# Two banded layers on one core: projections on 64 rows in pairs, with the bias in the weights

## The chip, the core and the metric

The kernel runs on one core of a Trainium2 chip. The metric is the time of one execution in device microseconds. The engines are called as in the profile: PE (TensorE matmul), PEld (TensorE weight load, recorded apart), DVE (VectorE), ACT (ScalarE), POOL (GpSimd), SP (SyncE, which here only issues DMAs).

## The reference

The input x is 512 x 512 positions with 64 channels, float32. Two layers of the same form follow each other, and each adds its result to x:

```python
xn = _ln(x, norm_scale, norm_bias)            # over the 64 channels; x is _gn(x) here
left = (xn @ Wl + bl) * mask * sigmoid(xn @ Wlg + blg)
right = (xn @ Wr + br) * mask * sigmoid(xn @ Wrg + brg)
out_gate = sigmoid(xn @ Wog + bog)
out = _banded_ingoing(left, right, 4)         # sum over 9 rows
out = _ln(out, out_norm_scale, out_norm_bias) * out_gate
return out @ Wo + bo
```

`_gn` is a group norm over all positions and groups of two channels. The five projections go from 64 to 128 channels. The banded sum takes, for output row i, the rows i-4 to i+4 of `right`, each times the entry of `left` at that row and column i: for each of the 128 hidden channels a product of a banded 512 x 512 matrix with a 512 x 512 matrix.

## The kernel before

The output rows are cut into blocks of 104 (the last has 96); 112 input rows go into each (`KIN`). Within a block the 512 columns are cut into 8 chunks of 64 columns. Two layers of five blocks of eight chunks make 80 chunks.

At the start of a block, `build_A` makes the band matrix A from `left`: 104 columns in 13 steps of 8 (`JP`). These are called band steps here. Then each chunk has two stages:

- `project` goes over its 64 columns in 8 steps of 8 columns. `transposed` turns the normalised z (rows in the partitions) on PE (line 274: four transposes, each of two columns of 64 channels, so that channels come out on 128 partitions), and ACT copies the result into the tile zT (line 281). `gated` multiplies four columns at a time with two weights side by side (line 288: the stationary operand is zT, 112 columns wide, the moving one the weights, 256 wide). ACT takes the sigmoid of one half (line 290), DVE multiplies it with the other and writes R (line 328). Line 332 makes the output gate with the gate's weights as the stationary operand and zT as the moving one, and line 337 its sigmoid.
- `mix` (line 346) multiplies A and R for each of 128 hidden channels; DVE and ACT empty PSUM into O in turns (lines 354 and 352).

`finish` is the third part. It takes the statistics of O (line 361 and the lines behind it), and then, in steps of 8 columns, normalises O (line 408, DVE), turns it (line 409, PE), scales it (line 411, ACT), multiplies it with the gates (line 412, DVE), multiplies with Wo (line 414, PE) and adds x (line 419, DVE). `together` emits `finish` of one chunk and `project` of the next in turns, so the two share a stage; `mix` stands alone. `normalised` prepares z, 16 columns at a time, over DMA, POOL, DVE and ACT, in two buffers.

The bias of a projection comes in as a 65th row: zT has a row of ones in partition 64, and the weights tile aug has the bias in partition 64. The lower 64 partitions of the transposed pair hold even columns, the upper 64 odd ones, and two ACT copies bring both to partitions 0 to 63.

A scheduler sets the order of instructions on each engine; every engine then runs its own list strictly in that order and waits where an operand is not ready. PSUM has four one-bank buffers (`one_bank`) and two of two banks (`two_banks`).

Of the kernel before, what the change touches and what calls it, by code (L numbers as in the profile page):

```python
# [8 lines left out]
F32 = mybir.dt.float32  # L9
# [47 lines left out]
class Block:  # L57
    """Rows o..o+m of the output; rows s..s+KIN go into them."""
# [9 lines left out]
def tile_two_banded_layers(  # L68
# [20 lines left out]
    # The first layer's output, less what its groups' means are near to: those of its input and  # L89
    # of the last bias. The second layer's norm does not see it, and its end adds it.  # L90
# [8 lines left out]

    def one_bank():  # L100
# [5 lines left out]
    def rsqrt(o: bass.AP, v: bass.AP):  # L106
        """o = v ** -0.5, for v > 0: a first guess from the bits of v, and Newton's steps."""
# [11 lines left out]
    def load_layer(i: int, w: dict, tmp) -> dict:  # L119
        r = {}  # L120
        raw = tmp.tile([D, 5 * H], F32, tag="raw", name=f"raw{i}")
        brow = tmp.tile([1, 5 * H], F32, tag="brow", name=f"brow{i}")
        for n, nm in enumerate(("r", "rg", "l", "lg", "og")):
            nc.sync.dma_start(raw[:, n * H : (n + 1) * H], w[f"W{nm}"])
            nc.sync.dma_start(brow[:, n * H : (n + 1) * H], row(w[f"b{nm}"]))
        ns = tmp.tile([D, 1], F32, tag="ns", name=f"ns{i}")
        nb = tmp.tile([D, 1], F32, tag="nb", name=f"nb{i}")
        nc.sync.dma_start(ns, col(w["norm_scale"]))
        nc.sync.dma_start(nb, col(w["norm_bias"]))
        aug = const.tile([D + 1, 5 * H], F32, tag=f"aug{i}", name=f"aug{i}")  # L130
        nc.vector.tensor_scalar(aug[:D, :], raw, ns, None, ALU.mult)
        for lo, hi in ((0, 4 * H), (4 * H, 5 * H)):
            pb = one_bank()
            nc.tensor.matmul(pb[:1, : hi - lo], lhsT=nb, rhs=raw[:, lo:hi], start=True, stop=True)
            nc.vector.tensor_tensor(brow[:, lo:hi], pb[:1, : hi - lo], brow[:, lo:hi], ALU.add)
        nc.sync.dma_start(aug[D : D + 1, :], brow)
# [6 lines left out]
        # To all partitions: the last bias, and the mask of the columns.  # L143
# [17 lines left out]
    def spread(o: bass.AP, v: bass.AP):  # L161
        """Values of the groups, [P, G], to their channels, [P, D]."""
# [6 lines left out]
    def group_affine(mean: bass.AP, var: bass.AP, pool):  # L169
        """From the groups' means and variances, on all partitions."""  # L170
# [351 lines left out]
```

## Time and profile before

| | |
|---|---|
| median of 2 runs | 16617.86 us (16617.22 to 16618.49) |
| profiled execution, first to last instruction | 16607.0 us; the profile gives no other time for it |
| busy time of PE | 14135.4 us |
| busy time of DVE | 9995.0 us |
| busy time of ACT | 4482.2 us |
| busy time of POOL | 4394.1 us |
| DMA | 521.69 MB, mean 31 GB/s |
| mean granted TensorE clock | 0.559 |

Rows of the grouped view read: line, engine, operation, output<-inputs, shape (for PE: rows * columns of the stationary operand, then the moving operand), count | busy us, mean ns of one | idle us of the engine before them, and what ended it. Rows of a view by stretches read: from:to in us, length, then busy us and count of PE, PEld, DVE, ACT and POOL, then the granted clock, the DMA share and GB/s. Rows of a timeline read: start, us, engine, line, operation, names, shape, count, and in brackets the idle time before it and what ended it; the us of several merged instructions run from the first start to the last end. A matmul's recorded end lies behind the start of the next, since matmuls are pipelined.

### The profile page before, as it was taken

The numbers are of one execution on the slowest core, as the hardware profiler recorded it, in microseconds if no ns is written. First come the engines' busy times: TensorE is split into PE (matmuls) and PEld (weight loads), VectorE is DVE, ScalarE is ACT, GpSimd is POOL, SyncE is SP. The second block draws the span as 40 slices with busy tenths as digits, with TensorE's granted clock in tenths as the row PEclk, the third lists the DMA queues.
The fourth block names the chain that finished last, engine by engine and source line by source line (L and its number), as shares of the span: only waits on it lengthen the run. The fifth ranks groups of instructions, "written<-read, shape, count | busy, mean of one in ns | idle before, by whom it ended". The sixth has DMA issues, their size and how long they took to land. (4 is left out here: it accounts for less than half of the span.)

```text
span 16607.0 us, 148858 instructions
## 1 busy us (share of the span) xinstructions
PE 14135.4 (85%) x53782; PEld 11229.3 (68%) x53782; DVE 9995.0 (60%) x24532; ACT 4482.2 (27%) x6982; POOL 4394.1 (26%) x2408
## 2 busy tenths in 40 slices
PE   3888888888888888888878888888888888888887
PEld 2677667666766676676657666666666766676776
DVE  7565665666566656656655555555555555556555
ACT  1222222222222222222222222222222222222222
POOL 2232422232223222422331113111311121113111
PEclk9999855555555555555555555555555555555555
DMA  4011101110111011100100111111011101110100
GB/s 177 24 30 27 30 26 28 27 31 25 28 27 31 25 27 27 31 25 26 31 25 26 27 29 29 27 29 29 27 29 29 29 26 30 27 30 27 29 27 27
DMA packets 130302, 521.69 MB, mean 31 GB/s; under 512 B 17872, under 2 KB 18522, under 8 KB 127516
## 3 DMA queue, kind: packets, MB, share of 16 engines
q1 hardware_dynamic: 129564, 512.18, 11.0%
q8 instruction: 423, 6.93, 0.2%
q14 instruction: 315, 2.58, 0.1%
HBM read 377.90 MB, written 134.22 MB: 31 GB/s over the span
## 5 line engine op out<-in xcount | busy, mean ns | idle before, releaser
L288 PE MATMUL banks<-aug,zT 65*112 65x256 f32 x12288 | 5734.7, 643 | 493.2 <-ACT zT L281 392.8
L288 PEld LDWEIGHTS banks<-aug,zT 65*112 65x112 f32 x12288 | 3619.6, 306 | 2234.2 <-ACT zT L281 629.9
L346 PE MATMUL bank<-R,A 112*104 112x64 f32 (+1 forms) x20480 | 3522.5, 378 | 4.0 <-DVE z_m L256 4.0
L346 PEld LDWEIGHTS bank<-R,A 112*104 112x104 f32 (+1 forms) x20480 | 3513.0, 290 | 16.4 <-DVE z_m L256 16.4
L414 PE MATMUL bank<-Wo,zh 128*104 128x64 f32 (+1 forms) x10240 | 1974.9, 377 | 1058.6 <-DVE zh L412 616.6
L414 PEld LDWEIGHTS bank<-Wo,zh 128*104 128x104 f32 (+1 forms) x10240 | 1899.9, 287 | 1352.1 <-issue 908.6
L252 POOL TENSOR_TENSOR z<-z,ga 112x1024 f32<-112x1024 f32 (+1 forms) x388 | 906.5, 2336 | 6161.5 <-DMA z<-mid_x 4155.6
L408 DVE TENSOR_SCALAR O<-O,o_nm,o_rs 104x128 f32<-104x128 f32 (+1 forms) x5120 | 2246.2, 490 | 0.6
L328 DVE TENSOR_TENSOR R<-banks,sg 112x512 f32<-112x512 f32 x1280 | 1321.0, 1032 | 1432.0 <-ACT sg L290 1428.8
L290 ACT ACTIVATE sg<-banks 112x512 f32<-112x512 f32 x1536 | 917.3, 597 | 4455.9 <-PE banks L288 4344.6
L354 DVE COPY O<-bank 104x512 f32<-104x512 f32 (+1 forms) x640 | 661.2, 1033 | 2292.8 <-PE bank L346 2290.8
L332 PE MATMUL bank<-zT,aug 65*128 65x416 f32 (+1 forms) x2560 | 2012.2, 889 | 0.0
L409 PEld LDWEIGHTS bank<-ident,O 104*128 104x128 f32 (+1 forms) x5120 | 959.5, 234 | 934.5 <-issue 772.1
L409 PE MATMUL bank<-ident,O 104*128 104x104 f32 (+1 forms) x5120 | 1130.4, 381 | 539.8 <-DVE O L408 539.8
L411 ACT ACTIVATE zh<-bank,ob,os 128x416 f32<-128x416 f32 (+1 forms) x1280 | 884.1, 692 | 2064.4 <-PE bank L409 2052.4
L352 ACT COPY O<-bank 104x512 f32<-104x512 f32 (+1 forms) x640 | 651.9, 1019 | 2921.8 <-PE bank L346 2921.8
L361 DVE BATCH_NORM_STATS2 o_st<-O 104x6 f32<-104x128 f32 (+1 forms) x5120 | 1136.7, 276 | 219.7 <-ACT O L352 219.7
L412 DVE TENSOR_TENSOR zh<-zh,gate 128x416 f32<-128x416 f32 (+1 forms) x1280 | 822.9, 643 | 737.6 <-ACT zh L411 729.1
L424 POOL TENSOR_TENSOR sum<-sum,xr 104x512 f32<-104x512 f32 (+1 forms) x320 | 431.5, 1348 | 2722.7 <-DVE xr L419 2064.8
L390 POOL TENSOR_TENSOR xr<-xr,add 104x1024 f32<-104x1024 f32 (+1 forms) x320 | 765.6, 2393 | 1356.0 <-DMA xr<-mid_x 798.8
L257 POOL TENSOR_TENSOR z<-z,z_m 112x1024 f32<-112x1024 f32 (+1 forms) x388 | 742.4, 1914 | 1329.9 <-DVE z_m L256 1067.7
L419 DVE TENSOR_TENSOR xr<-bank,xr 104x512 f32<-104x512 f32 (+1 forms) x640 | 441.9, 690 | 1059.9 <-PE bank L414 1052.0
(99 smaller groups left out, 10223.3 us busy)
## 6 DMA issues: line engine op xcount, KB each, us to landing
z<-in_x_dram SPq DMA_DIRECT2D x190, 448.0 KB
z<-mid_x SPq DMA_DIRECT2D x190, 448.0 KB
gn_x<-in_x_dram SPq DMA_DIRECT2D x16, 4096.0 KB
xr<-in_x_dram SPq DMA_DIRECT2D x128, 416.0 KB
mid_x<-xr SPq DMA_DIRECT2D x128, 416.0 KB
xr<-mid_x SPq DMA_DIRECT2D x128, 416.0 KB
out_dram<-xr SPq DMA_DIRECT2D x128, 416.0 KB
xr<-in_x_dram SPq DMA_DIRECT2D x32, 384.0 KB
```

The costliest lines, as they stand in the source:

```text
L252: nc.gpsimd.tensor_tensor(z, z, mid(ga[:KIN], n), ALU.mult)
L288: nc.tensor.matmul(pr[:KIN, q, :], lhsT=t[:, j + q, :], rhs=w, start=True, stop=True)
L290: nc.scalar.activation(sg, pr[:KIN, :, H:], AF.Sigmoid)
L328: nc.vector.tensor_tensor(R[:KIN, :, jr : jr + JQ].rearrange("p h j -> p j h"), v, sg, ALU.mult)
L332: nc.tensor.matmul(pg, lhsT=w["gate"], rhs=t[:, q : q + JQ, blk.off : blk.off + blk.m], start=True, stop=True,)
L346: nc.tensor.matmul(pb[:, h, :], lhsT=A[:KIN, h0 + h, : blk.m], rhs=R[:KIN, h0 + h, :], start=True, stop=True,)
L361: nc.vector.bn_stats(st[:, j, :], O[:m, j0 + j, :])
L408: nc.vector.tensor_scalar(oj, oj, nm[:, js], rs[:, js], ALU.add, ALU.mult)
L409: nc.tensor.transpose(pt[:, k * m : (k + 1) * m], oj, ident[:m, :m])
L411: nc.scalar.activation(zh, pt, AF.Identity, bias=w["ob"], scale=w["os"])
L412: nc.vector.tensor_tensor(zh, zh, gates[(j0 + q) // JQ], ALU.mult)
L414: nc.tensor.matmul(po[:, q + k, :], lhsT=zh[:, k * m : (k + 1) * m], rhs=w["Wo"], start=True, stop=True,)
```

## The change

Products use 64 rows of the array instead of 65. The transposed pair of columns stays where the transposes put it, even columns in partitions 0 to 63 and odd ones in 64 to 127, and one ACT instruction takes all 128 partitions. The weights lie twice in aug, once in each half, and the products of an even and an odd column alternate; those of even columns go to one PSUM bank of the pair, those of odd columns to the other.

The bias has no row any more. z has zero mean over its 64 channels, so the mean over the channels can be taken from each column of the weights without changing the product. ACT adds 1 to z on its way into zT, and the centred weights get the bias divided by 64 in each row: the ones times the weights then give the bias. The setup works this out with the block-diagonal tile half.

Since even and odd columns come apart, R and A are written in two DVE instructions, two columns each, where one wrote four, and the POOL multiplication of the band is split in the same way. The output gates of a step are made after both groups of products, one for the four even columns and one for the four odd ones, and `finish` takes the columns in that order.

Line numbers move: 274 becomes 289, 281 becomes 294, 288 becomes 306, 290 becomes 311, 328 becomes 354, 332 becomes 361, 337 becomes 366, 346 becomes 375, 361 becomes 390, 408 becomes 437, 409 becomes 438, 411 becomes 440, 412 becomes 441, 414 becomes 443.

```diff
     def load_layer(i: int, w: dict, tmp) -> dict:
...
-        raw = tmp.tile([D, 5 * H], F32, tag="raw", name=f"raw{i}")
+        raw = tmp.tile([P, 5 * H], F32, tag="raw", name=f"raw{i}")
...
+        for e in range(2):
+            part = slice(e * D, (e + 1) * D)
+            for n, nm in enumerate(("r", "rg", "l", "lg", "og")):
+                nc.sync.dma_start(raw[part, n * H : (n + 1) * H], w[f"W{nm}"])
...
-        aug = const.tile([D + 1, 5 * H], F32, tag=f"aug{i}", name=f"aug{i}")
-        nc.vector.tensor_scalar(aug[:D, :], raw, ns, None, ALU.mult)
+        nc.vector.tensor_scalar(brow, brow, 1.0 / D, None, ALU.mult)
+        hb = tmp.tile([P, P], F32, tag="hb", name=f"hb{i}")
+        nc.vector.tensor_scalar(hb, half, nb, None, ALU.mult)
+        aug = const.tile([P, 5 * H], F32, tag=f"aug{i}", name=f"aug{i}")
+        nc.vector.tensor_scalar(aug, raw, ns, None, ALU.mult)
         for lo, hi in ((0, 4 * H), (4 * H, 5 * H)):
-            pb = one_bank()
-            nc.tensor.matmul(pb[:1, : hi - lo], lhsT=nb, rhs=raw[:, lo:hi], start=True, stop=True)
-            nc.vector.tensor_tensor(brow[:, lo:hi], pb[:1, : hi - lo], brow[:, lo:hi], ALU.add)
-        nc.sync.dma_start(aug[D : D + 1, :], brow)
+            pm = one_bank()[:, : hi - lo]
+            nc.tensor.matmul(pm, lhsT=half, rhs=aug[:, lo:hi], start=True, stop=True)
+            pb = one_bank()[:, : hi - lo]
+            nc.tensor.matmul(pb, lhsT=hb, rhs=raw[:, lo:hi], start=True, stop=False)
+            nc.tensor.matmul(pb, lhsT=ones_row, rhs=brow[:, lo:hi], start=False, stop=True)
+            nc.vector.tensor_tensor(aug[:, lo:hi], aug[:, lo:hi], pm, ALU.subtract)
+            nc.vector.tensor_tensor(aug[:, lo:hi], aug[:, lo:hi], pb, ALU.add)
...
-    zT = [keep.tile([D + 1, JP // 2, 2, KIN], F32, name=f"zT{i}") for i in range(2)]
-    for t in zT:
-        nc.vector.memset(t[D : D + 1, :, :, :], 1.0)
+    zT = [keep.tile([P, JP // 2, KIN], F32, name=f"zT{i}") for i in range(2)]
...
     def transposed(z: bass.AP, j: int):
...
-        pt = pt[:, : JP // 2 * KIN].rearrange("q (k p) -> q k p", p=KIN)
-        for e in range(2):
-            nc.scalar.copy(t[:D, :, e, :], pt[e * D : (e + 1) * D])
-        return t.rearrange("c k e p -> c (k e) p")
+        nc.scalar.activation(
+            t.rearrange("c k p -> c (k p)"), pt[:, : JP // 2 * KIN], AF.Identity, bias=1.0
+        )
+        return t
 
     def gated(t: bass.AP, j: int, w: bass.AP):
-        pr = two_banks()
-        for q in range(JQ):
-            nc.tensor.matmul(pr[:KIN, q, :], lhsT=t[:, j + q, :], rhs=w, start=True, stop=True)
...
+        pr = two_banks().rearrange("p (e k) h -> p e k h", e=2)
+        for k in range(JQ // 2):
+            for e in range(2):
+                part = slice(e * D, (e + 1) * D)
+                nc.tensor.matmul(
+                    pr[:KIN, e, k, :], lhsT=t[part, j // 2 + k, :], rhs=w[part],
+                    start=True, stop=True,
+                )
...
     def build_A(zs, w: dict, mask: bass.AP, blk: Block):
...
-                    nc.gpsimd.tensor_tensor(sg, sg, last(b[:, i : i + JQ], H), ALU.mult)
-                    nc.vector.tensor_tensor(
-                        A[:KIN, :, i : i + JQ].rearrange("p h i -> p i h"), v, sg, ALU.mult
-                    )
+                    for e in range(2):
+                        nc.gpsimd.tensor_tensor(
+                            sg[:, e], sg[:, e], last(b[:, i + e : i + JQ : 2], H), ALU.mult
+                        )
+                        nc.vector.tensor_tensor(
+                            A[:KIN, :, i + e : i + JQ : 2].rearrange("p h k -> p k h"),
+                            v[:, e], sg[:, e], ALU.mult,
+                        )
...
     def project(zs, w: dict, blk: Block, gates: list):
...
-                    nc.vector.tensor_tensor(
-                        R[:KIN, :, jr : jr + JQ].rearrange("p h j -> p j h"), v, sg, ALU.mult
-                    )
-                    pg = one_bank()[:, : JQ * blk.m].rearrange("h (j p) -> h j p", p=blk.m)
+                    for e in range(2):
+                        nc.vector.tensor_tensor(
+                            R[:KIN, :, jr + e : jr + JQ : 2].rearrange("p h k -> p k h"),
+                            v[:, e], sg[:, e], ALU.mult,
+                        )
+                for e in range(2):
+                    part = slice(e * D, (e + 1) * D)
+                    pg = one_bank()[:, : JQ * blk.m].rearrange("h (k p) -> h k p", p=blk.m)
                     nc.tensor.matmul(
-                        pg, lhsT=w["gate"], rhs=t[:, q : q + JQ, blk.off : blk.off + blk.m],
+                        pg, lhsT=w["gate"][part], rhs=t[part, :, blk.off : blk.off + blk.m],
...
     def finish(src: bass.AP, dst: bass.AP, w: dict, blk: Block, c: int, gates: list, stats: bool):
...
-            for q in range(0, JP, JQ):
+            for e in range(2):
...
-                    j = j0 + q + k
+                    j = j0 + 2 * k + e
```

The scheduler puts the instructions nearly as before. These are the rows of PE in one step of the first layer, a finish step woven into a project step, before (L409 and L414 belong to the finish, the others to the projection):

```order
L409 MATMUL bank<-ident,O 128x104 x4
L274 MATMUL bank<-ident,z 128x112 x4
L288 MATMUL banks<-aug_101,zT_808 112x256
L414 MATMUL bank<-Wo_110,zh 104x64 x4
L288 MATMUL banks<-aug_101,zT_808 112x256 x3
L332 MATMUL bank<-zT_808,aug_101 128x416
L288 MATMUL banks<-aug_101,zT_808 112x256 x4
L332 MATMUL bank<-zT_808,aug_101 128x416
L409 MATMUL bank<-ident,O 128x104 x4
L414 MATMUL bank<-Wo_110,zh 104x64 x4
```

and in the changed kernel:

```order
L438 MATMUL bank<-ident,O 128x104 x4
L289 MATMUL bank<-ident,z 128x112 x4
L306 MATMUL banks<-aug_115,zT_845 112x256
L443 MATMUL bank<-Wo_131,zh 104x64 x4
L306 MATMUL banks<-aug_115,zT_845 112x256 x7
L361 MATMUL bank<-zT_845,aug_115 128x416 x2
L438 MATMUL bank<-ident,O 128x104 x4
L443 MATMUL bank<-Wo_131,zh 104x64 x4
```

The two gates have moved behind all eight products; the finish stands where it stood. L306 and L361 are of 64 rows, the rows around them of the whole array.

On DVE, at the head of a chunk's stage, the statistics of the first 32 columns of O (L361, now L390) stand between the writes of R, before:

```order
L361 BN_STATS o_st<-O 104x6 x15
L328 TENSOR_TENSOR R<-banks,sg 112x4x128
L361 BN_STATS o_st<-O 104x6 x10
L328 TENSOR_TENSOR R<-banks,sg 112x4x128
L361 BN_STATS o_st<-O 104x6 x8
```

and in the changed kernel:

```order
L390 BN_STATS o_st<-O 104x6 x15
L354 TENSOR_TENSOR R<-banks,sg 112x2x128 x2
L390 BN_STATS o_st<-O 104x6 x5
L354 TENSOR_TENSOR R<-banks,sg 112x2x128 x2
L390 BN_STATS o_st<-O 104x6 x13
```

Each write of R is two of half the size, and the second pair stands five statistics earlier.

More of the change, by code (lines that the diff above doesn't have):

```diff
@@ L98, in tile_two_banded_layers @@
     nc.vector.memset(ones_row, 1.0)
+    half = const.tile([P, P], F32, name="half")
+    nc.vector.memset(half, 0.0)
+    for e in range(2):
+        nc.vector.memset(half[e * D : (e + 1) * D, e * D : (e + 1) * D], 1.0 / D)
     def one_bank():
@@ L402, in finish @@
             po = one_bank()[:m, :].rearrange("i (j c) -> i j c", c=D)
-            for q in range(0, JP, JQ):
+            for e in range(2):
                 pt = one_bank()[:, : JQ * m]
                 for k in range(JQ):
-                    j = j0 + q + k
+                    j = j0 + 2 * k + e
                     oj, js = O[:m, j, :], slice(j % JS, j % JS + 1)
@@ L411, in finish @@
                 nc.scalar.activation(zh, pt, AF.Identity, bias=w["ob"], scale=w["os"])
[L412 removed]
+                nc.vector.tensor_tensor(zh, zh, gates[j0 // JQ + e], ALU.mult)
                 for k in range(JQ):
                     nc.tensor.matmul(
[L415 removed]
+                        po[:, 2 * k + e, :], lhsT=zh[:, k * m : (k + 1) * m], rhs=w["Wo"],
                         start=True, stop=True,
```

19 lines of the change are left out of this document (8 added, 11 removed).

## The prediction

> **What bounds the kernel now.** I read the page first, then the busy time by stretches, then TensorE's own timeline.
>
> ```profile
> span 16607.0 us, 148858 instructions
> PE 14135.4 (85%) x53782; PEld 11229.3 (68%) x53782; DVE 9995.0 (60%) x24532; ACT 4482.2 (27%) x6982; POOL 4394.1 (26%) x2408
> L288 PE MATMUL banks<-aug,zT 65*112 65x256 f32 x12288 | 5734.7, 643 | 493.2 <-ACT zT L281 392.8 <-DVE A L314 44.0 <-DVE z_r L116 25.4
> L288 PEld LDWEIGHTS banks<-aug,zT 65*112 65x112 f32 x12288 | 3619.6, 306 | 2234.2 <-ACT zT L281 629.9 <-issue 473.0 <-DVE A L314 51.8
> ```
>
> PE is busy 85%, and the largest group is the one that the change touches. The code has 6,144 of these products and the trace 12,288 records: each float32 product is two load-and-multiply records, one after the other.
>
> The stretches below are, in turn, the mixing stage of a chunk at an early and a later time, the project-and-finish stage of a chunk in the first and the second layer, and the two halves of a block's first chunk with its band.
>
> ```profile
> 649.60:695.50 45.90, 45.90 (x268) 45.90 (x267) 12.84 (x18) 8.28 (x9) 9.50 (x6) 1.00 0.08 20
> ...
> 6182.70:6228.60 45.90, 45.90 (x268) 45.90 (x267) 12.84 (x18) 8.28 (x9) 9.49 (x6) 0.50 0.07 19
> 6228.60:6372.70 144.10, 119.55 (x376) 86.70 (x376) 104.73 (x265) 45.78 (x75) 46.80 (x27) 0.50 0.12 31
> ...
> 10761.30:10904.00 142.70, 119.66 (x378) 86.87 (x377) 97.22 (x272) 41.66 (x68) 31.48 (x14) 0.50 0.12 31
> 6798.50:6935.00 136.50, 102.25 (x350) 79.18 (x349) 113.48 (x264) 39.37 (x63) 64.89 (x44) 0.50 0.11 30
> 6935.00:7063.10 128.10, 112.05 (x276) 75.71 (x276) 71.51 (x119) 39.41 (x68) 54.59 (x31) 0.50 0.11 31
> ```
>
> A chunk is 45.9 us of mixing, which the change leaves alone, and 144 us of projecting one chunk while the last one is finished. There are 80 chunks; 70 look like this and 10 open a block. The granted clock is 1.00 in the first row and 0.50 in the second, with the same 45.90 us: these matmuls do not follow it, and I give the clock no term. What ends last in the 144 us is seen in one step (8 columns) of PE's timeline:
>
> ```profile
> 6261.29 0.90 PE L409 MATMUL bank<-ident,O 104*128 104x104 f32 x4
> 6261.98 0.95 PE L274 MATMUL bank<-ident,z 112*128 112x112 f32 x4
> 6263.55 1.19 PE L288 MATMUL banks<-aug,zT 65*112 65x256 f32 x2 [0.61 <-ACT zT L281]
> 6264.54 1.52 PE L414 MATMUL bank<-Wo,zh 128*104 128x64 f32 x8
> 6265.85 2.85 PE L288 MATMUL banks<-aug,zT 65*112 65x256 f32 x6
> 6268.49 1.59 PE L332 MATMUL bank<-zT,aug 65*128 65x416 f32 x2
> 6269.88 3.62 PE L288 MATMUL banks<-aug,zT 65*112 65x256 f32 x8
> 6273.29 1.59 PE L332 MATMUL bank<-zT,aug 65*128 65x416 f32 x2
> 6274.68 0.90 PE L409 MATMUL bank<-ident,O 104*128 104x104 f32 x4
> 6277.09 1.62 PE L414 MATMUL bank<-Wo,zh 128*104 128x64 f32 x8 [1.51 <-DVE zh L412]
> 6278.50 0.90 PE L409 MATMUL bank<-ident,O 104*128 104x104 f32 x4
> ```
>
> From L409 to L409 the step takes 17.21 us, and PE's queue in order is the whole of it: the starts give 0.69 + 1.57 + 0.99 + 1.31 + 2.64 + 1.39 + 3.41 + 1.39 + 2.41 + 1.41. Two waits lie in it, for zT (inside the 1.57) and for zh (inside the 2.41). A record of L288 costs 3.41/8 = 0.426 us, one of L332 1.39/2 = 0.695 us; each ends about 0.21 us after the next has started (6269.88 + 3.62 against 6273.29), so the means on the page overstate PE. The projections are 16 x 0.426 + 4 x 0.695 = 9.6 of the 17.21 us.
>
> **Overlap of the halves.** Afterwards a product takes 64 rows, alternately the lower and the upper. The two records of one product stay in one half and must follow each other, but the second record of one product can run beside the first of the next. The order has one product alone, L443, seven products, two gates. Seven products are 14 records with 6 such meetings: 8 x 0.426 = 3.41 us, where 2.64 + 3.41 = 6.05 stood. The gates (four records of 0.695, one meeting of their own, and one with the last product) take 2.78 - 0.695 - 0.426 = 1.66 instead of 2.78. Together 3.76 us less per step. It needs the weights in time:
>
> ```profile
> 6246.31 3.62 PE L288 MATMUL banks<-aug,zT 65*112 65x256 f32 x8
> 6246.31 2.87 PEld L288 LDWEIGHTS banks<-aug,zT 65*112 65x112 f32 x7 [0.39 <-issue]
> ```
>
> Seven loads lie inside eight matmuls of the same rows, so a load runs beside the matmul ahead of it. A load that bounds its stream costs 45.90/268 = 0.171 us for 104 columns in the mixing rows, 0.184 for 112; two of them, 0.37, fit beside one record of 0.426. That two halves compute at once is shown by no row: the gain lies between 0 and 3.76, and I take the upper end: by the code the two products of a pair have their own partitions of zT and of the weights and their own PSUM bank, so that no data or buffer makes one wait for the other.
>
> [...]
>
> **Changes of tile size.** Products and gates now stand in another tiling than everything else on PE. Counted in the changed order, PE changes 2,248 times, four times in such a step; the one between L289 and L306 lies in the wait for zT. The nearest row is in the setup:
>
> ```profile
> 8.92 2.29 PE L134 MATMUL bank<-raw,nb 64*1 64x512 f32 x4 [8.92 <-DMA Wo<-in_L_conv_Wo_dram]
> 11.13 0.69 PE L151 MATMUL bank<-bo,ones_row 1*128 1x64 f32 x2
> ```
>
> L134 (64 rows) ends at 11.21 and L151 (1 row) starts at 11.13, 0.08 us before that end, where 0.21 is usual: 0.13 us lost. Behind a stop the first record also shows its load: L288 x2 lasts 0.99 above, 0.14 over 2 x 0.426. I take 0.27 us for each of three changes, 0.81 per step. Bounds: 0.13, and the whole tail with a whole load, 0.21 + 0.306 = 0.52.
>
> [...]
>
> **One copy instead of two, two products instead of one.**
>
> ```profile
> L328 DVE TENSOR_TENSOR R<-banks,sg 112x512 f32<-112x512 f32 x1280 | 1321.0, 1032 | 1432.0 <-ACT sg L290 1428.8
> ...
> L281 ACT COPY zT<-bank 64x448 f32<-64x448 f32 x1536 | 812.3, 529 | 187.7 <-PE bank L274 146.6
> ...
> L337 ACT ACTIVATE gate<-bank 128x416 f32<-128x416 f32 x1024 | 529.6, 517 | 742.5 <-PE bank L332 607.8 <-DVE zh L412 133.3
> ...
> L114 DVE TENSOR_TENSOR rsqrt<-z_r 112x16 f32<-112x16 f32 x1140 | 256.9, 225 | 13.3
> ```
>
> Two copies of 529 ns on 64 partitions become one on 128. The nearest row on 128, L337, takes 517, so PE's wait for zT shrinks by one copy, 0.53 us. R's evacuation becomes two of 256 elements. If DVE's time were all elements nothing would be added; if all of the 225 ns of a 16-element row were fixed, 0.22 each. I take 0.15: 0.3 us per step, 2.4 per chunk of DVE. The band's multiplications on POOL and DVE split alike, in 128 of 768 steps. The setup gets more loads and matmuls in front of the first transfer of x; the loads of now end by 8.92, so 0 to 10 us, taken as 5.
>
> **What the path keeps.** PE's step: 17.21 - 3.76 - 0.53 + 0.81 = 13.7 us, 3.5 less. But now DVE is near. Its busy time in the six steps behind the head:
>
> ```profile
> 6262.54:6279.75 17.21, 15.09 (x50) 11.06 (x49) 12.51 (x32) 5.30 (x10) 2.48 (x2) 0.50 0.01 1
> 6279.75:6296.97 17.22, 15.10 (x51) 11.07 (x49) 13.81 (x30) 5.32 (x10) 9.73 (x6) 0.50 0.29 77
> 6296.97:6315.65 18.68, 15.09 (x51) 11.08 (x49) 14.70 (x41) 6.14 (x11) 4.17 (x3) 0.50 0.00 1
> 6315.65:6328.35 12.70, 12.09 (x35) 8.35 (x33) 10.51 (x12) 4.10 (x8) 7.13 (x4) 0.50 0.39 103
> 6328.35:6345.00 16.65, 13.72 (x43) 9.63 (x41) 15.91 (x36) 5.06 (x9) 4.21 (x2) 0.50 0.00 0
> 6345.00:6362.00 17.00, 14.39 (x46) 10.36 (x46) 4.97 (x7) 4.97 (x9) 9.01 (x5) 0.50 0.10 28
> ```
>
> With 0.3 added, DVE (the third busy column) lets these steps save 3.5, 2.9, 3.5, 1.8, 0.4 and 3.4 us: 15.5, of which I keep 13 for queueing in its strict order. The second layer, with 97.22 instead of 104.73 us of DVE, keeps about 17 of 5 x 3.5 + 4.4. Ahead of the steps lies the head:
>
> ```profile
> 6228.39 0.95 PE L274 MATMUL bank<-ident,z 112*128 112x112 f32 x4
> ...
> 6239.80 0.95 PE L274 MATMUL bank<-ident,z 112*128 112x112 f32 x4
> ...
> 6256.46 1.11 PE L409 MATMUL bank<-ident,O 104*128 104x104 f32 x4 [5.15 <-DVE O L408]
> ```
>
> Two steps of 11.41 us run without a finish, then PE waits for DVE. A step there sheds 7 x 0.426 = 2.98, 1.12 on the gates and 0.53, and pays one change: 4.4 us. DVE's statistics, in turn, wait for the next z, whose buffer the second step frees; so the head gives one step's gain, 4.4, and the rest is waited away.
>
> A common chunk saves 17.4 in the first layer and 21.4 in the second, 19.4 on the mean. A block's first chunk: its first half is DVE's already (113.48 of 136.5), 3 us; in the second, eight steps without a finish at 4.4 and about three of the band at 3.2 make 45, of which I take three quarters, 33, since z tiles come from a chain over DMA, POOL, DVE and ACT that gets no faster. So 70 x 19.4 + 10 x 36 - 5 = 1,713 us off the profiled 16,607.0. The runs' median lies 11 us above that span: 14,894 + 11, say **14,900 us**. Its own range, with 12 to 27 us per common chunk and 20 to 50 per first one: 14,250 to 15,600.
>
> **Rivals.**
> *The weights come late.* For: no row shows a load passing a waiting matmul of the other half. Then each product's start waits for one load behind the last record: a pair of products takes 2 x (0.426 + 0.184) = 1.22, where now 1.70 and ideally 0.85. That is 56% of 3.76; a step saves 2.1 + 0.53 - 0.81 = 1.8, a chunk 10, a first chunk 20: 900 us, 15,720. Were a half's own load (0.306) never hidden, a pair takes 1.46, a step saves 0.8, a chunk about 5: 16,150. Against: the overlap of loads shown. Chance 0.13. [...]
>
> *DVE takes the step over.* For: 15.91 of 16.65. If POOL's interference and the extra instructions leave a chunk 9 and a first chunk 20: 15,790. Against: 4.97 of 17.00 one step on. Chance 0.09.
>
> *The halves do not compute at once* (the change doesn't do what it says). Then only the copies and the changes of tiling count: -768 x 0.53 = -407, and 2,248 x 0.27 = +607: 16,820, within 2% (332 us, about what a measurement of this kernel can tell from no change). Chance 0.09.
>
> *The same, and each change of tiling drains and reloads*, on the other side: 2,248 x 0.52 = 1,169 - 407 = +762, 17,380. It decides from (332 + 407)/2,248 = 0.33 us a change; were the halves to overlap it would take 1.2 us. For it: nothing in the steady stages shows a change yet. Against: 0.13 us in the setup. Chance 0.15.
>
> **Chances and range.** Forecast 0.54, the first two rivals 0.22: faster 0.76; within 2% 0.09; slower 0.15. Leaving out the slow case and the low tail, the range is 14,250 to 16,900.
>
> **What would show it.** Starts of neighbouring L306 records about 0.43 us apart in pairs that coincide, 3.4 us for seven products, prove the overlap; even spacing of 0.426 refutes it, 0.6 between pairs means late weights. L306 to L443 shows the price of a change. L289 to L306 should be 1.04 us. Steps of 13.7 us prove the sum; steps of 16 with DVE busy throughout prove DVE. What would make it wrong at once is a period of a chunk of 190 us or more.

## The result, and the profile after

The changed kernel takes 15059.37 us (median of 2 runs, 15052.18 to 15066.56) against 16617.86: a ratio of 0.9063, 95% interval 0.9037 to 0.9089. The forecast was 14,900 us. The profiled execution's span went from 16607.0 to 15064.8 us, 1,542 us less, where the sum had 1,713.

From the page of the changed kernel, the span and the busy time of the engines:

```profile
span 15064.8 us, 150188 instructions
...
PE 10365.6 (69%) x53798; PEld 8549.5 (57%) x53798; DVE 9972.1 (66%) x26077; ACT 3944.5 (26%) x6214; POOL 4445.0 (30%) x2664
```

PE is busy 3,770 us less, and less than half of that is gone from the span. DVE, which did not change, is now at 66%, about level with PE. The grouped view shows the products, and the two instructions that write R and normalise O:

```profile
L306 PE MATMUL banks<-aug,zT 64*112 64x256 f32 x12288 | 2973.0, 599 | 986.5 <-ACT zT L294 358.3 <-DVE R L354 232.0 <-DVE A L338 165.6
L437 DVE TENSOR_SCALAR O<-O,o_nm,o_rs 104x128 f32<-104x128 f32 (+1 forms) x5120 | 2244.9, 488 | 1.6
L354 DVE TENSOR_TENSOR R<-banks,sg 112x256 f32<-112x256 f32 x2560 | 1321.9, 589 | 209.5 <-ACT sg L311 205.2
```

The products fell from 5,734.7 to 2,973.0 us of busy time. R's 2,560 half writes cost 1,321.9 us, where 1,280 whole ones cost 1,321.0: splitting them was free.

The stretches of the changed kernel that answer to those of before: the mixing, the project-and-finish stage in the first and in the second layer, and a block's first chunk with its band in one row.

```profile
5722.60:5768.50 45.90, 45.90 (x267) 45.90 (x266) 12.77 (x18) 8.40 (x9) 9.55 (x6) 0.50 0.07 20
5768.50:5899.70 131.20, 80.52 (x377) 59.36 (x376) 103.04 (x281) 40.16 (x67) 46.82 (x27) 0.62 0.12 33
10043.30:10165.50 122.20, 78.07 (x378) 57.52 (x377) 96.05 (x288) 35.67 (x60) 31.59 (x14) 0.61 0.13 36
6301.10:6528.80 227.70, 122.72 (x626) 85.98 (x624) 188.59 (x421) 65.44 (x110) 124.47 (x99) 0.63 0.13 35
```

Mixing stays at 45.90 us. The first layer's stage went from 144.1 to 131.2 us, the second's from 142.7 to 122.2, the first chunk's two stretches from 136.5 + 128.1 to 227.7. In the first layer PE is busy for only 80.5 of 131.2 us: it waits. The granted clock, 0.50 in these stages before, is now 0.6 on the mean in those with projections.

PE's timeline at the start of such a stage and in one step of it:

```profile
5770.03 3.76 PE L306 MATMUL banks<-aug,zT 64*112 64x256 f32 x16 [0.74 <-ACT zT L294]
5773.58 1.60 PE L361 MATMUL bank<-zT,aug 64*128 64x416 f32 x4
5775.11 0.78 PE L289 MATMUL bank<-ident,z 112*128 112x112 f32 x4
5776.62 1.98 PE L306 MATMUL banks<-aug,zT 64*112 64x256 f32 x16 [0.73 <-ACT zT L294]
5778.44 0.86 PE L361 MATMUL bank<-zT,aug 64*128 64x416 f32 x4
...
5796.18 0.90 PE L438 MATMUL bank<-ident,O 104*128 104x104 f32 x4
5796.87 0.95 PE L289 MATMUL bank<-ident,z 112*128 112x112 f32 x4
5798.46 1.19 PE L306 MATMUL banks<-aug,zT 64*112 64x256 f32 x2 [0.63 <-ACT zT L294]
5799.58 1.65 PE L443 MATMUL bank<-Wo,zh 128*104 128x64 f32 x8
5801.15 3.33 PE L306 MATMUL banks<-aug,zT 64*112 64x256 f32 x13
5803.85 0.90 PE L361 MATMUL bank<-zT,aug 64*128 64x416 f32 x1
5804.27 0.63 PE L306 MATMUL banks<-aug,zT 64*112 64x256 f32 x1
5804.55 1.74 PE L361 MATMUL bank<-zT,aug 64*128 64x416 f32 x3
5806.22 0.58 PE L438 MATMUL bank<-ident,O 104*128 104x104 f32 x4
5809.96 1.62 PE L443 MATMUL bank<-Wo,zh 128*104 128x64 f32 x8 [3.15 <-DVE zh L441]
5811.37 0.90 PE L438 MATMUL bank<-ident,O 104*128 104x104 f32 x4
```

Sixteen records take 3.55 us from start to start (5770.03 to 5773.58): eight times 0.427 and a change of tiling, so the halves compute at once from the first record to the last. One step later the same sixteen take 1.82 us. That is about half of it, and nothing in the code differs. In the step from 5796.18 to 5811.37 the projections, which there run at the old rate, cost what was forecast, but the wait for zh has grown from 1.51 to 3.15 us. These two readings, the halved records and the longer waits, are what the experiments were for.

### The profile page after: what moved, and what is told of

Its sections match the earlier page's. It is cut to its first block, busy times and chain, and to the rows that moved or that the text cites. A ratio compares the mean times of both kernels' runs of the same rounds, so it can differ in the third digit from the quotient of the medians.

```text
span 15064.8 us, 150188 instructions
## 1 busy us (share of the span) xinstructions
PE 10365.6 (69%) x53798; PEld 8549.5 (57%) x53798; DVE 9972.1 (66%) x26077; ACT 3944.5 (26%) x6214; POOL 4445.0 (30%) x2664
## 5 line engine op out<-in xcount | busy, mean ns | idle before, releaser
L306 PE MATMUL banks<-aug,zT 64*112 64x256 f32 x12288 | 2973.0, 599 | 986.5 <-ACT zT L294 358.3
L375 PE MATMUL bank<-R,A 112*104 112x64 f32 (+1 forms) x20480 | 3522.2, 378 | 64.1 <-DVE R L354 64.1
L443 PE MATMUL bank<-Wo,zh 128*104 128x64 f32 (+1 forms) x10240 | 1955.4, 373 | 2039.2 <-DVE zh L441 842.6
L443 PEld LDWEIGHTS bank<-Wo,zh 128*104 128x104 f32 (+1 forms) x10240 | 1766.8, 276 | 2464.1 <-issue 1834.0
L306 PEld LDWEIGHTS banks<-aug,zT 64*112 64x112 f32 x12288 | 1761.5, 273 | 1706.7 <-ACT zT L294 598.5
L437 DVE TENSOR_SCALAR O<-O,o_nm,o_rs 104x128 f32<-104x128 f32 (+1 forms) x5120 | 2244.9, 488 | 1.6
L438 PE MATMUL bank<-ident,O 104*128 104x104 f32 (+1 forms) x5120 | 1013.8, 348 | 1085.5 <-DVE O L437 1085.1
L438 PEld LDWEIGHTS bank<-ident,O 104*128 104x128 f32 (+1 forms) x5120 | 800.1, 207 | 1448.0 <-issue 1041.7
L354 DVE TENSOR_TENSOR R<-banks,sg 112x256 f32<-112x256 f32 x2560 | 1321.9, 589 | 209.5 <-ACT sg L311 205.2
L390 DVE BATCH_NORM_STATS2 o_st<-O 104x6 f32<-104x128 f32 (+1 forms) x5120 | 1134.7, 278 | 221.0 <-ACT O L381 221.0
L441 DVE TENSOR_TENSOR zh<-zh,gate 128x416 f32<-128x416 f32 (+1 forms) x1280 | 765.9, 601 | 486.2 <-ACT zh L440 478.2
L274 ACT ACTIVATE sq<-z 112x1024 f32<-112x1024 f32 (+1 forms) x388 | 405.7, 1046 | 2013.0 <-POOL z L272 2010.3
```

The source lines that it names most:

```text
L306: nc.tensor.matmul(pr[:KIN, e, k, :], lhsT=t[part, j // 2 + k, :], rhs=w[part], start=True, stop=True,)
L354: nc.vector.tensor_tensor(R[:KIN, :, jr + e : jr + JQ : 2].rearrange("p h k -> p k h"), v[:, e], sg[:, e], ALU.mult,)
L375: nc.tensor.matmul(pb[:, h, :], lhsT=A[:KIN, h0 + h, : blk.m], rhs=R[:KIN, h0 + h, :], start=True, stop=True,)
L390: nc.vector.bn_stats(st[:, j, :], O[:m, j0 + j, :])
L437: nc.vector.tensor_scalar(oj, oj, nm[:, js], rs[:, js], ALU.add, ALU.mult)
L438: nc.tensor.transpose(pt[:, k * m : (k + 1) * m], oj, ident[:m, :m])
```

## Experiments

| run | what differs | us | mean granted clock |
|---|---|---|---|
| e1_lower_half | all products on the same 64 rows | 16864.08 | 0.502 |
| e2_full_rows | products on 128 rows, half of them zeros | 15134.47 | 0.677 |
| e3_wide_mix | changed kernel, mixing 104 columns wide | 13481.39 | 0.691 |
| e7_mix_80 | the same, 80 wide | 15067.10 | 0.593 |
| e11_mix_92 | the same, 92 wide | 13656.39 | 0.670 |
| e6_before_wide_mix | kernel before, mixing 104 wide, first run | 31340.35 | 0.581 |
| e9_before_wide_again | kernel before, mixing 104 wide | 14781.88 | 0.605 |
| e10_rows_wide | e2 and e3 together | 13654.66 | 0.763 |
| e5_no_sums | changed kernel without POOL's sums | 14668.04 | 0.595 |
| e4_act_norm | half of O's normalisation on ACT | 14567.49 | 0.600 |
| e8_wide_act | e3 and e4 together | 13009.87 | 0.691 |
| e12_wide_act34 | e8 with three quarters on ACT | 12864.32 | 0.689 |

Where the text gives no number of runs, the time is that of a single one. Time ahead of a trace's first clock record counts as 1.00 in the means (12,958 us of e6, under 0.5 ms elsewhere in the table).

The theories: the halves overlap (the forecast), or the gain comes from somewhere else; and the part of the gain that is missing is PE's own, or DVE's, or comes from POOL.

**Is it the overlap? All products on the lower rows.** ACT makes two copies, one for each parity, both into partitions 0 to 63; every product and gate uses those rows.

```diff
-    zT = [keep.tile([P, JP // 2, KIN], F32, name=f"zT{i}") for i in range(2)]
+    zT = [keep.tile([D, 2, JP // 2, KIN], F32, name=f"zT{i}") for i in range(2)]
...
-                    pr[:KIN, e, k, :], lhsT=t[part, j // 2 + k, :], rhs=w[part],
+                    pr[:KIN, e, k, :], lhsT=t[:, e, j // 2 + k, :], rhs=w[:D],
```

> The changed kernel with every product on the lower 64 rows, and with two copies into zT as before; the bias stays in the weights, and the order and the changes of tiling stay. Theory (the gain is the overlap of the two halves): without a second half at work the records of L306 follow each other at 0.43 us, PE pays 2,248 changes at about 0.14 to 0.27 us for nothing, and the time is 16,700 to 17,000. Rival (the gain comes from fewer waits and the new order of gates): most of the gain stays, 15,300 to 15,600.

16864.08 us. PE's timeline of this run, and that of the weight loads:

```profile
6005.66 7.17 PE L306 MATMUL banks<-aug,zT 64*112 64x256 f32 x16
6005.66 6.42 PEld L306 LDWEIGHTS banks<-aug,zT 64*112 64x112 f32 x16
```

Sixteen records take 7.17 us instead of 3.76: one after the other, each 0.427. The gain is gone when the halves are gone. The loads of these records (the second row) stay hidden beside the products though all use the same rows (6.42 us of loads within the 7.17), which speaks against the rival in which a half's own load is never hidden.

**Or the share of the array? 128 rows, no halves.** The weights stand twice in a zero-padded tile, so that a product takes all 128 rows of zT and the zeros drop the other column. Nothing overlaps and no tiling changes.

```diff
+        pad = const.tile([P, 2, 5 * H], F32, tag=f"pad{i}", name=f"pad{i}")
+        nc.vector.memset(pad, 0.0)
+        for e in range(2):
+            part = slice(e * D, (e + 1) * D)
+            nc.vector.tensor_copy(pad[part, e, :], aug[part, :])
...
-                    pr[:KIN, e, k, :], lhsT=t[part, j // 2 + k, :], rhs=w[part],
+                    pr[:KIN, e, k, :], lhsT=t[:, j // 2 + k, :], rhs=w[:, e, :],
```

> The changed kernel with products over all 128 rows: the weights lie twice, each time with zeros in the other half, so there is no change of tiling and no pair, but one copy into zT, the halved writes of R and the gates at the end of the step stay. One gate buffer fewer, to make room. Theory (overlap): products are serial again, a common chunk sheds 8 x 0.5 us of the copy, 16,250 to 16,400, with L306 at 0.43 us. Rival (the gain is the full clock, which PE is granted once all of its rows are in use): L306 falls to 0.21 us for part of the time here too, the granted clock rises to 0.6 or more, and the time is 15,000 to 15,500.

15134.47 us, only 75 us more than with the halves. PE's timeline, two steps in turn:

```profile
5809.38 5.82 PE L311 MATMUL banks<-pad,zT 128*112 128x256 f32 x16 [0.74 <-ACT zT L300]
...
5817.64 3.71 PE L311 MATMUL banks<-pad,zT 128*112 128x256 f32 x16 [0.66 <-ACT zT L300]
```

The first sixteen records begin at 0.427 us each and end at 0.216, the second sixteen run at 0.216 throughout. So TensorE does have a faster rate here, twice the usual one, and full rows reach it with zeros in half of them. In this trace the clock's own records show 1.00 in 556 windows, 5,339 us in all; in the changed kernel in 581 windows of 3.4 to 13.7 us, 2,761 us; in the kernel before in three, 17 us. The change thus brings two things, an overlap that holds at either clock (sixteen records in 3.55 us at 0.50, in 1.82 at 1.00) and bursts of the full clock. The full clock without the overlap brings nearly the same time; whether the overlap alone would is not shown, and how much of the 1,542 us is the clock's share was not separated: no run had the overlap at 0.50 throughout. The trace of the changed kernel bounds it. A fifth of L306's records (2,512 of 12,288) start at 1.00, where 7,293 do with full rows, and PE is busy for 1,068 of the 2,761 us at 1.00. Even if all of that would have taken twice as long at 0.50 (an estimate), at least some 2,700 of the 3,770 us that PE is busy less are not the clock's.

**Does the mixing follow the clock?** It is 45.9 us of every chunk, and if the share of the array in use decides, it should be possible to raise it. In the changed kernel each mixing product now reads 104 moving columns instead of 64; the 40 more land where the next product of the bank writes, which overwrites them.

```diff
-                    pb[:, h, :], lhsT=A[:KIN, h0 + h, : blk.m], rhs=R[:KIN, h0 + h, :],
+                    pf[:, h * JC : h * JC + n], lhsT=A[:KIN, h0 + h, : blk.m],
+                    rhs=Rf[:KIN, (h0 + h) * JC : (h0 + h) * JC + n],
```

with n = 104, and 64 for the last product of a bank.

> The changed kernel with 104 instead of 64 moving columns in the mixing products: the 40 further columns are written over by the next product of the same bank, so that the output is the same. The records are bound by their weight loads of 104 columns, so that this costs nothing by itself. If the granted clock follows how much of the array is in use: the mixing stage (0.50 now) gets the full clock, 45.9 us become 23 to 30, and the time is 13,300 to 14,000. If it does not: 45.9 us as before, 15,050 to 15,150.

13481.39 us, 1,578 us faster for 40 useless columns. PE's timeline of a mixing stage in this run:

```profile
4839.42 3.54 PE L378 MATMUL bank<-R,A 112*104 112x104 f32 x20
...
4843.49 21.80 PE L378 MATMUL bank<-R,A 112*104 112x104 f32 x236
```

Twenty records at 0.17 us, the old rate, then 236 at 0.092. Where the change of rate lies, the next two runs narrow down (the same edit with other widths):

> As the changed kernel with the wide mix, but with 80 moving columns instead of 104. Of the array's rows times columns times time, mixing then uses 112/128 x 80/128 = 0.55, where 64 columns use 0.44 and 104 use 0.71. If the clock goes up where a threshold under 0.55 is passed: about 13,480 as with 104. If the threshold is above: 15,060. In between, if the share of windows with the full clock follows the use gradually: 13,900 to 14,700.

> The changed kernel with mixing products of 92 moving columns. 80 columns gave nothing (15067 us), 104 gave 13481 us. Rows x columns in use times the share of time: 112/128 x 92/104 of the time of a weight load is 0.77 against 0.67 (80) and 0.875 (104). Theory A, a limit below 0.77: mixing runs at the full clock, near 13,500 us. Theory B, a limit above it: mixing stays at 0.173 us a record, 15,070 us. Anything between would mean that the clock goes up and down within a mixing stage.

```profile
L378 PE MATMUL bank<-R,A 112*104 112x92 f32 (+3 forms) x20480 | 2159.0, 275 | 54.8 <-DVE R L354 54.8
```

80 columns change nothing (15067.1 us); 92 do nearly all of it (13656.39 us, the grouped row above, against 3,522.2 us for the mixing of the changed kernel). At the old rate a record takes 0.17 us with 64 moving columns and with 104, so the load of 104 columns sets it. A loaded column then costs 0.171/104 = 1.65 ns, a moving one 0.427/256 = 1.67 ns (from L306), so 80 columns keep the array computing about 77% of the time, 92 columns 88% (an estimate from these two). The step lies between.

**The same edit on the kernel before.** A first run of it took 31340.35 us. Its page shows the clock by slices, and the products:

```profile
PEclk9999999999999999622222222222222222333333
...
L288 PE MATMUL banks<-aug,zT 65*112 65x256 f32 x12288 | 11794.5, 1221 | 384.3 <-ACT zT L281 381.8 <-DVE A L314 2.5
```

> The kernel before with 104 instead of 64 moving columns in its mixing products, nothing else. Theory (full clock once enough of the array is in use, whatever else the kernel does): mixing falls from 45.9 to about 24 us, the projections stay at 0.43 us a record, since they use 65 rows, and the time is 14,700 to 15,000. Rival (it takes the pairs of halves in the stage before to raise the clock): 16,600.

The records of L288 are spaced 1.28 us at first, then 0.84 and at last 0.62, where 0.427 is usual; the 9s stand where no grant was recorded (the first 12,958 us), and the two grants on record behind that are 0.26 and 0.36. The same code was run once more:

> The kernel before with mixing products of 104 moving columns, once more. The earlier run of the same code took 31340 us, with a clock of a quarter to a third where it was recorded. Theory A, that slowness belonged to that run: mixing goes to the full clock as in the changed kernel with the same edit (0.092 us a record instead of 0.173), a chunk loses 15 to 22 us, 80 chunks 1,200 to 1,800 us: 14,800 to 15,400 us. Theory B, it belongs to this program: 31,000 us again, with the projections' records of 65 rows spaced 1.28 us at first and 0.6 to 0.85 later.

14781.88 us (2 runs; ratio 0.8897, 95% interval 0.8871 to 0.8922). So the slowness does not belong to the program. The repeat ran on another chip, and other programs had their usual times on the first one; what caused it stays open. PE's timeline of the repeat, a mixing stage and the projections behind it:

```profile
5205.04 21.80 PE L349 MATMUL bank<-R,A 112*104 112x104 f32 x236
...
5228.31 2.10 PE L288 MATMUL banks<-aug,zT 65*112 65x256 f32 x8 [1.08 <-ACT zT L281]
...
5263.06 3.62 PE L288 MATMUL banks<-aug,zT 65*112 65x256 f32 x8
```

With the projections of before, one edit in the mixing gains more than the whole change: the mixing runs at the full clock, the first products behind it too (eight records in 2.10 us), later ones at 3.62 as ever. The change is worth 1,300 us on top of it (14,782 to 13,481).

**Do the halves still count at the full clock?** Full rows and wide mixing together:

> Full 128-row products one after the other (no overlap, no change of tile size) with the mixing products at 104 moving columns. The pairs with the same mixing took 13481 us. Theory A, the clock carries the gain and the overlap hardly counts, since DVE sets the step once PE runs at the full clock: 13,450 to 13,700 us. Theory B, the overlap is a gain of its own on top of the clock: seven products cost 14 x 0.213 instead of 8 x 0.213 us and the gates two records more, about 1.8 us a step less 0.4 us of tile changes at the higher clock, 768 steps: 13,481 + 1,000, 14,300 to 14,700 us.

13654.66 us (ratio 0.8218, 95% interval 0.8194 to 0.8242), 173 us above the halves with the same mixing: theory A. In the grouped view PE's largest wait of this run ends with DVE:

```profile
L451 PE MATMUL bank<-Wo,zh 128*104 128x64 f32 (+1 forms) x10240 | 1777.0, 347 | 1710.9 <-DVE zh L449 1325.6 <-DVE z_v L284 161.2 <-DVE z_m L277 148.4
```

With the pairs (e3) the products are busy for 1,018 us less (2,850.4 instead of 3,868.5), and PE waits 326 us longer at that place (2,036.9 instead of 1,710.9).

**What holds the first layer back: POOL's sums.** The two additions that POOL makes per step in the first layer are left out except in the first step of a block; the running sums, and so the second layer's group norm, are not the reference's.

```diff
-                nc.gpsimd.tensor_tensor(sum1[:m], sum1[:m], f, ALU.add)
-                nc.gpsimd.tensor_tensor(sum2[:m], sum2[:m], s2, ALU.add)
+                if c == 0 and j0 == 0:
+                    nc.gpsimd.tensor_tensor(sum1[:m], sum1[:m], f, ALU.add)
+                    nc.gpsimd.tensor_tensor(sum2[:m], sum2[:m], s2, ALU.add)
```

The reason to suspect them stands in DVE's timeline of the changed kernel,

```profile
5807.96 1.35 DVE L437 TENSOR_SCALAR O<-O,o_nm,o_rs 104x128 f32<-104x128 f32 x5
...
5824.56 1.22 DVE L270 TENSOR_REDUCE z_m<-z 112x16 f32<-112x1024 f32 x1 [2.57 <-POOL z L268]
5825.70 0.58 DVE L441 TENSOR_TENSOR zh<-zh,gate 128x416 f32<-128x416 f32 x1
...
5849.40 7.54 DVE L437 TENSOR_SCALAR O<-O,o_nm,o_rs 104x128 f32<-104x128 f32 x5
```

and in POOL's at the same places:

```profile
5818.52 1.27 POOL L454 TENSOR_TENSOR sum<-sum,s 104x512 f32<-104x512 f32 x1
5819.74 2.37 POOL L267 TENSOR_TENSOR z<-z,ga 112x1024 f32<-112x1024 f32 x1
5822.19 2.34 POOL L268 TENSOR_TENSOR z<-z,gb 112x1024 f32<-112x1024 f32 x1
...
5849.63 1.27 POOL L453 TENSOR_TENSOR sum<-sum,xr 104x512 f32<-104x512 f32 x1 [12.11 <-DVE xr L448]
5850.86 1.27 POOL L454 TENSOR_TENSOR sum<-sum,s 104x512 f32<-104x512 f32 x1
5852.08 2.36 POOL L267 TENSOR_TENSOR z<-z,ga 112x1024 f32<-112x1024 f32 x1
5854.52 2.34 POOL L268 TENSOR_TENSOR z<-z,gb 112x1024 f32<-112x1024 f32 x1
```

Five normalisations that take 1.35 us alone take 7.54 while POOL works through four instructions; DVE goes on when POOL is done (POOL's last ends at 5856.86, the fifth normalisation at 5856.94). And at 5824.56 DVE has waited 2.57 us for z, which POOL prepared behind its sums; zh, for which PE waits, stands behind that in DVE's order. Why an instruction on POOL holds up one on DVE, these rows do not show.

> The changed kernel without POOL's additions into the sums of the first layer's output, but for a few at each block's start (so the second layer's norm is not the reference's). Theory (POOL's instructions hold up DVE's, and DVE ends PE's waits for zh): a common chunk of the first layer takes about 169 us as in the second, where it takes 177.4 now, and the time is 14,700 to 14,800. Rival (the first layer is slower for another reason): 15,000 to 15,060.

14668.04 us, 391 us less. In the grouped view of this run:

```profile
L437 DVE TENSOR_SCALAR O<-O,o_nm,o_rs 104x128 f32<-104x128 f32 (+1 forms) x5120 | 2118.0, 464 | 0.6
```

L437 costs 127 us less (2,244.9 to 2,118.0), the lines of the reciprocal roots (L116 to L121; in the changed kernel one of 16 elements takes 1.26 us at 5835.05, beside a sum on POOL, where its like takes 0.17) 250 us less together. DVE's busy time fell by 381 us (to 9,590.8) and the span by 398. On the mean a common chunk now takes 166.6 us in the first layer and 166.3 in the second, where the changed kernel has 175.8 and 166.4: the sums are what sets the first layer apart. They act on two ways, by holding up DVE and by standing ahead of z in POOL's order, and the run does not separate the two. The edit was not tried on the kernel before. There the layers are only 1.2 us a chunk apart (188.4 and 187.2), so the sums can have cost little then (an estimate from that difference).

**DVE itself.** Every second group of O (the odd columns) is normalised on ACT, with the bias worked out beside the statistics:

```diff
-                    nc.vector.tensor_scalar(oj, oj, nm[:, js], rs[:, js], ALU.add, ALU.mult)
+                    if e == 1:
+                        nc.scalar.activation(oj, oj, AF.Identity, bias=nr[:, js], scale=rs[:, js])
+                    else:
+                        nc.vector.tensor_scalar(oj, oj, nm[:, js], rs[:, js], ALU.add, ALU.mult)
```

> The changed kernel with every second group of four columns of O normalised on ACT instead of DVE (L437), which takes about 14 of 103 busy us of a stage off DVE. Theory (behind the change DVE's queue, held up by POOL, ends PE's waits for zh): a chunk sheds 4 to 10 us, 14,300 to 14,750. Rival (PE's own chain in its order is the bound): the time stays within 100 us of 15,060, or rises since ACT answers later.

14567.49 us, 492 less: taking work off DVE gains, in a kernel whose busiest engine by the page is PE.

**Both together, and further.** The wide mixing with this normalisation, and then also with the odd ones of the even groups on ACT (`if e == 1 or k % 2`):

> The changed kernel with the wide mix and with every second group of O normalised on ACT, the two edits that gained 1,580 and 490 us one by one. If PE's clock and DVE's queue are separate limits, the gains add: 12,950 to 13,100. If mixing at the full clock leaves DVE as the bound of nearly all, taking work off DVE gains more than alone: 12,500 to 12,900.

> The kernel with 104-column mixing and half of O's normalisation on ACT took 13010 us with DVE 8996 us (69%) and ACT 4933 us (38%). Here three quarters go to ACT: another 1,280 instructions of 0.47 us leave DVE (-600 us) and 1,280 of 0.41 us come to ACT (+530). Theory A, DVE still sets the steps: 12,700 to 12,850 us. Theory B, the first ACT instruction of a group now stands ahead of its sigmoid and zh work in ACT's order, so that the chain from O to zh waits for ACT instead: 12,950 to 13,200 us.

13009.87 us (4 runs; ratio 0.7833, 95% interval 0.782 to 0.7847): the two gains add (1,578 and 472 of 492). The last one is the fastest of all, 12864.32 us (4 runs, 12851.72 to 12868.8; ratio 0.774, 95% interval 0.7727 to 0.7753):

```profile
PE 8549.8 (66%) x53798; PEld 6842.2 (53%) x53798; DVE 8091.8 (63%) x22397; ACT 5400.1 (42%) x10054; POOL 4444.4 (35%) x2664
```

It misses theory A's range by 14 us: of 904 us that left DVE's busy time (8,996.2 to 8,091.8), 146 left the span. No engine is over two thirds busy any more; what is left are waits between them.

## Why the prediction was right, point by point

*What bounds the kernel.* Right for PE's queue, and its terms can be checked one by one in the step from 5796.18 to 5811.37, beside the one of 17.21 us:

| stretch | before | forecast | after |
|---|---|---|---|
| L438 to L289 | 0.69 | 0.69 | 0.69 |
| L289 to L306 (zT) | 1.57 | 1.04 | 1.59 |
| lone product | 0.99 | 0.99 + 0.27 | 1.12 |
| L443 | 1.31 | 1.31 + 0.27 | 1.57 |
| seven products and gates | 8.83 | 5.07 + 0.27 | 5.07 |
| L438 and L443 | 3.82 | 3.82 | 5.15 |
| sum | 17.21 | 13.73 | 15.19 |

*The overlap*, taken at its upper end, was exact: 5.07 us, and a change of tiling within it. The clock has no part in this, since all projections of this step ran at 0.50 (the full clock came from 5806.24 to 5809.65, in the wait for zh). The halves do even more than was reckoned. At 5803.85 a gate's record starts in the lower half, 0.42 us before the last product's record starts in the upper: the half that had finished its own went on alone, ahead of a record that stands before it in PE's list. The list was not kept strictly in order across the halves.

*The changes of tiling* were over-priced. The lone product takes 0.13 us more than before, the eight L443 0.26 more (0.12 at their first record and 0.14 behind their last, by the single records), and the one behind the gates 0.14 by the gates' spacing, which the freer halves make up for. That is 0.13 to 0.26 us a change, and the step pays 0.39 where 0.81 was taken. The rival of 0.52 us each is refuted.

*One copy instead of two*, 0.53 us a step, was wrong. ACT's timeline, before and after:

```profile
6262.97 1.08 ACT L281 COPY zT<-bank 64x448 f32<-64x448 f32 x2
```

```profile
5797.86 0.54 ACT L294 ACTIVATE zT<-bank 128x448 f32<-128x448 f32 x1
```

The first product before started at 6263.55, as soon as the first of the two copies was done; the second lay beside the lone product and L414. In this step PE did not wait for both. So a gain of 0.53 was missing, and 0.42 of tiling was not paid: PE's queue sheds 3.35 us instead of 3.48, right by two errors that nearly cancel.

*The clock.* "These matmuls do not follow it" is the sentence that fell. The 1.00 in the first row of before was no grant: the trace of before has no clock record ahead of 1,956 us, and the 45.90 us was the half rate in both rows (at 1.00 a mixing stage of 64 columns takes 23.60 us, e2). The page's mean of 0.559 counts that time as 1.00 too. It carried no term, but the rule behind it was wrong, and it hid a gain as large as the forecast one (e9).

*DVE's bounds.* This step is the one that was mis-sized. The steps behind the head, of 17.2, 17.2 and 18.7 us before, are now, by stretches (the fourth row holds two of them):

```profile
5796.18:5811.37 15.19, 11.40 (x51) 8.08 (x50) 12.19 (x35) 4.68 (x8) 2.49 (x2) 0.61 0.00 0
5811.37:5827.84 16.47, 10.68 (x50) 7.94 (x50) 9.98 (x30) 4.47 (x8) 8.49 (x5) 0.60 0.31 81
5827.84:5843.74 15.90, 8.55 (x50) 6.57 (x50) 15.05 (x45) 5.41 (x9) 5.38 (x4) 0.71 0.00 1
5843.74:5872.60 28.86, 17.72 (x74) 11.89 (x74) 26.39 (x57) 7.68 (x13) 11.36 (x6) 0.62 0.17 46
```

They save 2.0 us, 0.7 and 2.8 instead of 3.5, 2.9 and 3.5 (the 2.9 should have been 3.1 by the row shown, 17.22 - 13.81 - 0.3). Neither PE nor DVE fills the second: DVE is busy 9.98 of 16.47 us, and the rows of 5824.56 show why. The sum allowed 2.5 us a chunk for such queueing. PE's idle time where L443 comes right behind L438 went from 482 to 1,034 us in the first layer and from 474 to 822 in the second; without POOL's sums (e5) the two layers have 830 and 824.

From mixing stage to mixing stage, on the mean, a common chunk is 12.6 us shorter in the first layer (188.4 to 175.8; forecast 17.4) and 20.8 in the second (187.2 to 166.4; forecast 21.4), a block's first chunk about 38 (forecast 36). The first layer's common chunks are short by 35 x 4.8 = 168 us, the second's by 21, and the first chunks with the setup give some 20 back: of the 171 us that are missing nearly all lie in the first layer, and e5 shows the cause that only the first layer has, POOL's sums. L437 cost 2,246.2 us before (as L408), held-up ones included, so POOL held this line up no less then. That it lay beside PE's queue at the time is argued, from the 1.2 us between the layers.

*The splits of R*, 0.15 us each, cost nothing. *The head* sheds 5.1 us (28.1 to 23.0 us from the stage's start to its first L438) against 4.4; its sixteen records take eight turns of 0.427, where nine were reckoned.

*The rivals.* Late weights: refuted, pairs coincide and come every 0.427 us. DVE takes over: half right, as the mechanism of the first layer at a fifth of its price. Halves not at once, with or without the dearer change of tiling: refuted by the pairs; e1, without them, took 16,864 us, near the 16,820 of the first, though by other terms: it keeps both copies, and pays less for tiling.

## What to carry to other kernels

Read the granted clock against the spacing of equal records before calling a matmul's time fixed: where a stage of back-to-back matmuls sits at half rate, use more of the array (both row halves, wider moving operands, even zeros or columns that are overwritten) and see whether the rate doubles, as it nearly did here from 0.427 to 0.216 us a record (e2) and from 0.17 to 0.092 (e3). Two products of 64 rows on the two halves ran as if alone here, a pair of records every 0.427 us, at 0.13 to 0.26 us for each change of tiling. And once PE sheds a fifth, look at whom its waits name next: a wait that lay beside PE's queue at little cost, DVE behind POOL here, comes out as span (391 us here, by e5).

## What the runs showed of the hardware

**In these runs the clock followed how much of the array was in use, not how busy PE was.** The mixing keeps PE busy 45.90 of 45.90 us and stays at 0.50. With the same loads and 104 instead of 64 moving columns it goes to 1.00 (e9, 5205.00 to 5226.80), in the stage of e3 after some 20 records (3.5 us). With 92 a record's median is 255 ns, as with 104; with 80 it is 381 ns, and the mean clock is 0.593, as with 64. Projections of 65 or 64 rows one after the other stayed at 0.50 by themselves (1.00 for 17 us in the kernel before, 24 in e1), while 128 rows and pairs of 64 went up (5,339 and 2,761 us at 1.00). Where the limit lies is known only between 80 and 92 columns for that stage.

**What was raised stayed raised in some stages.** In the full-rows kernel the mixing of 64 columns ran at either rate, by what stood ahead of it (two mixing stages, by stretches):

```profile
4768.70:4814.60 45.90, 45.90 (x267) 45.90 (x266) 9.48 (x10) 8.88 (x10) 8.76 (x6) 0.50 0.08 19
5061.40:5085.00 23.60, 23.60 (x258) 23.60 (x259) 13.34 (x24) 8.27 (x9) 4.22 (x2) 1.00 0.01 1
```

The second stands in a block's first chunk, behind steps without a finish, whose products take most of PE's time. Eight of the ten first chunks mix in under 24 us, none of the other 70 does.

**The two halves had their own order.** In the changed kernel the records of a pair start at the same time to within 0.01 us, and a half did not wait for the other's older record (5803.85 against 5804.27).

**One execution ran TensorE's projections at a third to two thirds of the usual half rate** (1.28 to 0.62 us a record against 0.427) for all its 31 ms, and the same program did not the next time; a single run with a surprising time is worth a second one.
